# A graph kernel with two neural layers: message sums and gates in one rotation of five PSUM banks, one set of transposes issued a step later

## The chip, the cores and the metric

The kernel runs on one core of a Trainium2 chip. Times are microseconds on the device; the metric is the time of the core for one execution. One more execution was recorded by the hardware profiler, and all views below are of that one.

## What is computed

Sixteen graphs of 1024 nodes with 128 features each pass through two layers. Layer 0 is a gated recurrent network of four steps: messages are summed over the adjacency, and a GRU cell updates the node states. Layer 1 first thins the adjacency in a sequential rule (each row's removals change later rows), then runs three graph convolutions with batch norm. Both layers end with a residual and a layer norm. Cut to what matters here:

```python
h = x
for i in range(4):
    hw = einsum('bnc,cd->bnd', h, weight[i])
    m = einsum('bjn,bjd->bnd', adj, hw)
    h = gru_cell(m, h, w_ih[i], w_hh[i], b_ih[i], b_hh[i])   # gates r, z, n
# the thinning, for each row n in turn:
num = sum(row); rank = cumsum(row)
sf = where(num > 10, (num + 1) // 2, 1)
rm = row & (rank % sf == 0)            # removed in row n and in column n
```

## The kernel before, in words

The program has a first part, to about 1550 us, in which the gated network (class Gated) and the thinning (class FixPoint) run side by side, and a second part (class Sage) with the convolutions. The change touches the first part alone.

**Gated.** Two graphs are in flight as streams 0 and 1. run (L1083) loops over pairs of graphs, the four layers, and the two streams, and calls layer (L1033) each time: 64 calls. A layer holds nodes as columns, in two halves f=0 and f=1 of 512. For each half it sums messages into a PSUM bank (L1045): 8 matmuls with the high part of the state (hi) and 8 with the low part (lo), and ScalarE copies the sum to SBUF (h_ms, L1048). Then come the gates of each half (gate, L1054; matmuls L1057). Their order on TensorE: the reset gate r (weights on h, then on m), the hidden part ph (h), the input part px (m), the update gate z (h, then m). A float32 matmul of 128x512 is two instructions in the records, so a group of r or z has four. The readers: sigmoid of r on ScalarE (L1066), VectorE's product with ph (L1070) and sum with px (L1072), tanh on ScalarE (L1073), sigmoid of z on ScalarE (L1076), then z times h on GpSimd (L1078), VectorE (L1079) and GpSimd (L1080), which writes the new state. While one stream is in its layer, the other's new state is transposed (turn, L992, matmuls L997) and split into hi and lo (L985, L990).

**FixPoint.** It handles four graphs at a time (G = 4), in blocks of 128 rows: 32 blocks, k = 0 to 7 in each group of four graphs. It is a generator (steps, L735) with 20 yields to the block. For each graph g it needs the removals of earlier blocks, which are transposed on TensorE into the PSUM tile f_tr (turn, L716, matmuls L723; k of them, none where k = 0), multiplied into the rows on VectorE (L730), and counted by a scan of 1024 on VectorE (L732); L730 and L732 are in count (L725). There is one f_tr for all graphs, so the transposes of a graph wait for the multiply of the graph before, and a multiply waits for its transposes. After the four scans come the sum per row (L799), the parameters (L687 to L702), an Abs on ScalarE (diag_u, L870, L874), the removals x on VectorE (removed, L878, L881, tile f_x), and a triangular matmul on TensorE (less, L885, L889), whose result corrects the counts.

**The order.** [...] A layer calls aside(n) for n = 0 to 9, and each call takes one step of the generator, so a block of FixPoint lies on two calls of layer, stream 0 and then stream 1. In the second: aside 1 (between the hi and lo sums of f=0) issues the transposes and the count of graph 1; aside 2 (ahead of the hi sums of f=1) those transposes of graph 2; aside 3 (between hi and lo of f=1) the count of graph 2; aside 4 (after the sums) transposes and count of graph 3, L799, the parameters and diag_u. Then come r, ph and px of f=0, aside 5 (removed, and the other stream's turn), z of f=0, aside 6 (less), and the gates of f=1 with asides 7 to 9. Asides 2 and 3 are where the change moves a step. Graphs are counted from 0 here.

**PSUM.** Of the eight banks, FixPoint has two (f_tr and f_pd). Gated has three in the pool h_ps1 (the sums h_m0 and h_m1, and the transposes h_tr) and three in h_ps3, through which the eight gate groups of a layer rotate as h_g. A group may write a bank only after the reader of the group three before has ended: the z group of a half takes the bank of its own r group, and waits for that sigmoid.

Of the kernel before, what the change touches and what calls it, by code (L numbers as in the profile page):

```python
# [8 lines left out]
F32 = mybir.dt.float32  # L9
BF = mybir.dt.bfloat16  # L10
F16 = mybir.dt.float16
FR = mybir.dt.float32r
F8 = mybir.dt.float8e4
I32 = mybir.dt.int32
U8 = mybir.dt.uint8
AF = mybir.ActivationFunctionType
# [3 lines left out]
PSUM = bass.MemoryType.PSUM  # L20
# [5 lines left out]
C = 128  # L26
NB = N // P
HF = 512
# [24 lines left out]
class Dilate:  # L53
# [152 lines left out]
    def steps(self):  # L206

        for b in range(B):
            self.load(0, b)
            yield 3.0  # L210
        for k in range(NB):
            self.start_chain(k)
            for t in range(P):
                self.chain_step(k, t)
                yield 1.9
            self.end_chain(k)
            x = {}
            for i in range(B + 3):
                if i < B:
                    x[i] = self.rank(k, i)  # L220
                if 1 <= i <= B:
                    self.remove(k, i - 1, x.pop(i - 1))
                if i >= 3 and k + 1 < NB:
                    self.load(k + 1, i - 3)
                yield 5.0
# [402 lines left out]
class FixPoint:  # L628
# [106 lines left out]
    def steps(self):  # L735

        nc, G = self.nc, self.G
        for c in range(self.LOTS):
            self.load(c)
        old = None  # L740
        for i, (k, b0) in enumerate(self.todo):
            diag = slice(k * P, k * P + P)
            after = slice(k * P + 1, k * P + 1 + P)

            yield
            if old:
                old.settle()
                old.wide_u(0)
            yield
            if old:  # L750
                old.wide_u(1)
                old.rows(0)
            yield
            if old:
                old.wide_u(2)
                old.rows(1)
            yield
            if old:
                old.rows(2)
                old.wide_u(3)  # L760
            a = [self.loaded.pop((i, g)) for g in range(G)]
            pt = self.ps.tile([P, G, P], F32, name="f_pd")
            for g in range(G):
                nc.tensor.transpose(pt[:, g, :], a[g][:, diag], self.cst["ident"])
            yield
            yield
            if old:
                old.rows(3)
                old.last_u()
            yield  # L770

            self.turn(i, 0)
            yield

            both = self.small.tile([P, G, P], BF, name="f_both")
            for g in range(G):
                nc.vector.tensor_mul(both[:, g, :], a[g][:, diag], pt[:, g, :])
            nc.gpsimd.affine_select(both, both, pattern=[[0, G], [1, P]], compare_op=ALU.is_gt, fill=0.0,
                                    base=0, channel_multiplier=-1)
            rank = self.two.tile([P, G, N + 2], F16, name="f_rank")  # L780
            nc.vector.tensor_copy(rank[:, :, 0], self.first[:, k, b0:b0 + G])
            self.count(i, 0, a[0], rank, pt)
            yield
            yield
            yield
            self.turn(i, 1)
            self.count(i, 1, a[1], rank, pt)
            yield
            self.turn(i, 2)
            yield  # L790
            self.count(i, 2, a[2], rank, pt)
            for g in range(G):
                self.read_back(i + 1, g)
            yield
            self.turn(i, 3)
            self.count(i, 3, a[3], rank, pt)

            num = self.sm[:, 0, 0, :]
            nc.vector.tensor_scalar(num, rank[:, :, N], 1.0, None, op0=ALU.mult)  # L799
            q = self.params(num, 0)  # L800
            u = self.diag_u(rank[:, :, after], q)
            if old:
                old.check()
            yield
            x = self.removed(u, q, both)
            yield
            pd, num = self.less(x, rank, 1)
            rd = self.small.tile([P, G, P], F16, name="f_rd")
            q = self.params(num, 1, lambda: nc.vector.tensor_sub(rd, rank[:, :, after], pd))
            yield  # L810
            u = self.diag_u(rd, q)
            yield
            x = self.removed(u, q, both)
            yield
            old = self.Block(self, i, a, rank, both, x)
            yield
        for n in range(4):
            if n == 0:
                old.settle()
            old.wide_u(n)  # L820
            old.rows(n)
        old.last_u()
        old.check()
# [81 lines left out]
class Gated:  # L905
# [7 lines left out]
    def __init__(self, ctx, tc, cst, x, adj, weight, w_ih, w_hh, b_ih, b_hh, summed):  # L913
        self.tc, self.nc, self.cst = tc, tc.nc, cst
        self.x, self.adj, self.summed = x, adj, summed
        nc = self.nc
        pool = lambda name, **k: ctx.enter_context(tc.tile_pool(name=name, **k))
        self.one = pool("h_one", bufs=1)
        self.adjp = pool("h_adj", bufs=NB)
        self.wk = pool("h_wk", bufs=2)  # L920
        self.ps1 = pool("h_ps1", bufs=1, space=PSUM)
        self.ps3 = pool("h_ps3", bufs=3, space=PSUM)
        self.wi = self.one.tile([C, L0, 3, C], F32, name="h_wi")
        self.wh = self.one.tile([C, L0, 3, C], F32, name="h_wh")
        self.bi = self.one.tile([C, L0 * 3], F32, name="h_bi")
        self.bh = self.one.tile([C, L0 * 3], F32, name="h_bh")
        self.bs = self.one.tile([C, L0 * 3], F32, name="h_bs")
        with tc.tile_pool(name="h_in", bufs=2) as wk:
            self.prepare(wk, weight, w_ih, w_hh, b_ih, b_hh)
# [102 lines left out]

    def layer(self, st, l, aside):  # L1033

        nc, wk, ps1 = self.nc, self.wk, self.ps1
        half = [slice(f * HF, (f + 1) * HF) for f in range(2)]
        pm = [ps1.tile([C, HF], F32, name=f"h_m{f}") for f in range(2)]
        ms = []
        for f in range(2):
            for n, part in enumerate((st.hi, st.lo)):  # L1040
                aside(2 * f + n)
                if l == 0 and f == 1 and n == 0:
                    st.begin(1)
                for j in range(NB):
                    nc.tensor.matmul(pm[f], part[:, j, :], st.adj[j][:, half[f]],  # L1045
                                     start=(j == 0 and n == 0), stop=(j == NB - 1 and n == 1))
            m = wk.tile([C, HF], F32, name="h_ms")
            nc.scalar.copy(m, pm[f])  # L1048
            ms.append(m)
        aside(4)  # L1050
        bias = lambda t, g: t[:, 3 * l + g:3 * l + g + 1]
        w = lambda t, g: t[:, l, g, :]

        def gate(*mm):  # L1054
            pg = self.ps3.tile([C, HF], F32, name="h_g")
            for i, (lhs, rhs) in enumerate(mm):
                nc.tensor.matmul(pg, lhs, rhs, start=(i == 0), stop=(i == len(mm) - 1))  # L1057
            return pg

        for f in range(2):  # L1060
            h, m = st.ht[:, half[f]], ms[f]
            r = wk.tile([C, HF], F32, name="h_r")
            z = wk.tile([C, HF], F32, name="h_z")
            zh = wk.tile([C, HF], F32, name="h_zh")
            pr = gate((w(self.wh, 0), h), (w(self.wi, 0), m))
            nc.scalar.activation(r, pr, AF.Sigmoid, bias=bias(self.bs, 0))  # L1066
            if f == 1:
                aside(7)
            ph = gate((w(self.wh, 2), h))
            nc.vector.scalar_tensor_tensor(r, ph, bias(self.bh, 2), r, op0=ALU.add, op1=ALU.mult)  # L1070
            px = gate((w(self.wi, 2), m))
            nc.vector.tensor_add(r, px, r)  # L1072
            nc.scalar.activation(r, r, AF.Tanh, bias=bias(self.bi, 2))  # L1073
            aside(5 if f == 0 else 8)
            pz = gate((w(self.wh, 1), h), (w(self.wi, 1), m))
            nc.scalar.activation(z, pz, AF.Sigmoid, bias=bias(self.bs, 1))  # L1076

            nc.gpsimd.tensor_tensor(zh, z, h, ALU.mult)  # L1078
            nc.vector.scalar_tensor_tensor(r, z, 1.0, r, op0=ALU.subtract, op1=ALU.mult)  # L1079
            nc.gpsimd.tensor_tensor(h, zh, r, ALU.subtract)  # L1080
            aside(6 if f == 0 else 9)

    def run(self, steps):  # L1083
# [17 lines left out]
        for _ in steps:  # L1101
            pass

    def beside(self, st, ot, l, s, b0, steps):


# [815 lines left out]
```

## Time and profile before

| what | us |
|---|---|
| median of three runs | 2795.58 (2790.15 to 2797.11) |
| the profiled execution, its own time | 2790.13 |
| its span, first to last instruction | 2788.4 |
| TensorE matmul busy | 2420.7 (87%) |
| VectorE busy | 1972.3 (71%) |
| ScalarE busy | 1365.7 (49%) |
| GpSimd busy | 1007.0 (36%) |

The mean granted clock of TensorE is 0.951 of full speed. In a timeline line, the first number is the start in us from the first instruction, the second the length; then engine (PE is TensorE's matmul, PEld its weight load, DVE VectorE, ACT ScalarE, POOL GpSimd, SP the engine that only issues DMAs), line of the kernel, operation, tile written and tiles read, shapes, and how many were merged. Square brackets give the idle time of the engine just before and what ended it. In the windows view, PEclk is the granted clock of TensorE in that stretch.

### The profile page before, as it was taken

How to read it: one execution, taken by the hardware profiler on the slowest of the kernel's cores; microseconds unless marked ns; L12 is line 12 of the kernel's file. 1: busy time of each engine (PE TensorE's matmuls, PEld its weight loads, DVE VectorE, ACT ScalarE, POOL GpSimd, SP SyncE). 2: the span in 40 equal slices, each digit the busy share in tenths (PEclk: the TensorE clock that was granted, in tenths of full speed). 3: DMA queues.
4: the chain of work that ended last, by engine and by line, in shares of the span. 5: the costliest groups of instructions: out<-in, count | busy, mean ns of one | idle time of the engine just before them, and what ended most of it. 6: DMA issues, size and time to landing. Idle time of an engine off the chain costs nothing.

```text
span 2788.4 us, 35994 instructions
## 1 busy us (share of the span) xinstructions
PE 2420.7 (87%) x12167; PEld 1616.0 (58%) x12167; DVE 1972.3 (71%) x4184; ACT 1365.7 (49%) x3094; POOL 1007.0 (36%) x938
## 2 busy tenths in 40 slices
PE   5998989898989898989898599999999889988765
PEld 2555555555555555555554367767766677766544
DVE  1887887878878878788788656565566466656666
ACT  1455545454545454545554455555545344533335
POOL 2234334252352442533532454445445344430000
PEclk9999999999999999999999799999999999999986
DMA  6135344171342442623530757665666266643213
GB/s 223 48 129 175 106 149 146 50 251 59 132 166 94 152 149 69 218 71 128 176 103 27 295 201 253 247 229 214 250 242 225 96 225 225 232 164 107 92 38 100
DMA packets 214396, 436.19 MB, mean 156 GB/s; under 512 B 59573, under 2 KB 80730, under 8 KB 214202
## 3 DMA queue, kind: packets, MB, share of 16 engines
q1 hardware_dynamic: 191162, 349.91, 36.5%
q0 software_dynamic: 23040, 83.90, 9.0%
q8 instruction: 98, 1.61, 0.2%
q14 instruction: 96, 0.79, 0.1%
HBM read 324.49 MB, written 109.25 MB: 156 GB/s over the span
## 4 chain that ended last, share of the span: by engine, by line
DVE 37%; PE 29%; ACT 20%; DMA 6%; issue 5%; POOL 2%; SPq 0%; DVEq 0%; ACTq 0%; POOLq 0%
DVE f_rank L732 11%; PE h_g L1057 7%; PE p_ag L1477 6%; ACT s_junk L1317 3%; ACT f_pd L874 3%; DVE h_r L1079 3%; DVE f_a L730 2%; DVE s_r L1328 2%; PE p_dg L1461 2%; ACT f_u L897 2%; PE q_ag L1701 2%; ACT f_u L900 2%; DVE h_r L1070 2%; ACT h_r L1066 2%; DVE h_r L1072 2%
## 5 line engine op out<-in xcount | busy, mean ns | idle before, releaser
L1057 PE MATMUL h_g<-h_h,h_wh 128*128 128x512 f32 x768 | 429.0, 642 | 108.8 <-ACT h_r L1066 108.8
L1078 POOL TENSOR_TENSOR h_zh<-h_z,h_h 128x512 f32<-128x512 f32 x128 | 195.5, 1527 | 653.1 <-ACT h_z L1076 653.0
L1057 PE MATMUL h_g<-h_ms,h_wi 128*128 128x512 f32 x768 | 412.9, 621 | 0.0
L1409 POOL CAST p_b<-p_at 128x512 uint8<-128x512 f32 x256 | 213.0, 851 | 250.3 <-ACT p_at L1402 227.3
L732 DVE TENSOR_TENSOR_SCAN f_rank<-f_a,f_first,f_pd 128x1024 f16<-128x1024 f32 x128 | 299.8, 2347 | 4.0
L1045 PE MATMUL h_m<-h_a,h_hi 128*128 128x512 f32 x1024 | 281.7, 417 | 0.0
L1057 PEld LDWEIGHTS h_g<-h_ms,h_wi 128*128 128x128 f32 x768 | 154.3, 201 | 200.4 <-issue 194.6
L1045 PE MATMUL h_m<-h_a,h_lo 128*128 128x512 f32 x1024 | 260.4, 396 | 0.8 <-POOL h_lo L1017 0.7
L1402 ACT ACTIVATE p_at<-p_u,s_less 128x512 fp32r<-128x512 f32 x256 | 175.1, 685 | 157.0 <-PE p_u L1401 153.6
L1057 PEld LDWEIGHTS h_g<-h_h,h_wh 128*128 128x128 f32 x768 | 134.9, 201 | 198.1 <-ACT h_r L1066 126.8
L851 DVE SCALAR_TENSOR_TENSOR f_nr<-f_u,f_q,f_a 128x1024 bf16<-128x1024 f16 x128 | 195.3, 1528 | 56.7 <-ACT f_u L900 47.5
L1045 PEld LDWEIGHTS h_m<-h_a,h_hi 128*128 128x128 f32 x1024 | 189.4, 189 | 62.2 <-issue 27.4
L1080 POOL TENSOR_TENSOR h_h<-h_zh,h_r 128x512 f32<-128x512 f32 x128 | 190.2, 1486 | 73.8 <-DVE h_r L1079 51.0
L1317 ACT ACTIVATE s_junk<-s_o 128x128 bf16<-128x128 f32 x384 | 113.6, 298 | 204.5 <-DVE s_o L1310 204.5
L1045 PEld LDWEIGHTS h_m<-h_a,h_lo 128*128 128x128 f32 x1024 | 187.7, 188 | 39.1 <-POOL h_lo L1017 1.9
L1415 DVE SCALAR_TENSOR_TENSOR p_junk<-p_a 128x1024 bf16<-128x1024 f32 x128 | 183.9, 1437 | 2.3
L1070 DVE SCALAR_TENSOR_TENSOR h_r<-h_g,h_bh,h_r 128x512 f32<-128x512 f32 x128 | 95.7, 748 | 111.8 <-ACT h_r L1066 83.4
L1073 ACT ACTIVATE h_r<-h_r,h_bi 128x512 f32<-128x512 f32 x128 | 92.4, 722 | 163.4 <-DVE h_r L1072 163.4
L1048 ACT COPY h_ms<-h_m 128x512 f32<-128x512 f32 x128 | 73.7, 576 | 197.7 <-PE h_m L1045 156.8
L897 ACT ACTIVATE f_u<-f_rank,f_q 128x128 f16<-128x128 f16 (+7 forms) x128 | 110.6, 867 | 96.4 <-DVE f_rank L837 96.4
L1079 DVE SCALAR_TENSOR_TENSOR h_r<-h_z,h_r 128x512 f32<-128x512 f32 x128 | 118.2, 924 | 53.2 <-ACT h_z L1076 53.2
L1400 PE MATMUL p_u<-ident_b,p_a 128*128 128x128 bf16 x1024 | 146.8, 223 | 4.4 <-DMA p_a<-in_adj_dram 4.4
(227 smaller groups left out, 5072.6 us busy)
## 6 DMA issues: line engine op xcount, KB each, us to landing
h_a<-in_adj_dram POOLq DMA_DIRECT2D x128, 512.0 KB, 6.7
f_a<-in_adj_dram SPq DMA_DIRECT2D x128, 512.0 KB
p_a<-in_adj_dram SPq DMA_DIRECT2D x128, 512.0 KB
e_nr<-f_nr SPq DMA_DIRECT2D x128, 256.0 KB
p_nr<-e_nr SPq DMA_DIRECT2D x32, 1024.0 KB
s_at<-p_b SPq DMA_DIRECT2D x32, 512.0 KB
s_rt<-s_rt SPq DMA_DIRECT2D x64, 256.0 KB
s_ag<-s_ag SPq DMA_DIRECT2D x64, 256.0 KB
```

The source lines that it names most:

```text
L732: nc.vector.tensor_tensor_scan(out, a, other[:, 0, 0:1].to_broadcast([P, N]), start, op0=ALU.add, op1=ALU.bypass)
L851: nc.vector.scalar_tensor_tensor(nr, self.us[g], self.q[:, 2, g:g + 1], self.a[g], op0=ALU.not_equal, op1=ALU.is_ge)
L1045: nc.tensor.matmul(pm[f], part[:, j, :], st.adj[j][:, half[f]], start=(j == 0 and n == 0), stop=(j == NB - 1 and n == 1))
L1057: nc.tensor.matmul(pg, lhs, rhs, start=(i == 0), stop=(i == len(mm) - 1))
L1078: nc.gpsimd.tensor_tensor(zh, z, h, ALU.mult)
L1079: nc.vector.scalar_tensor_tensor(r, z, 1.0, r, op0=ALU.subtract, op1=ALU.mult)
L1080: nc.gpsimd.tensor_tensor(h, zh, r, ALU.subtract)
L1317: self.nc.scalar.activation(junk, o[:, i, :], AF.Square, accum_out=ss[:, i:i + 1])
L1402: nc.scalar.activation(g["at"][:, j, cols], pu, AF.Relu, bias=self.less2)
L1409: self.nc.gpsimd.tensor_copy(g["b", f][:, j, :], g["at"][:, j, f * HF:(f + 1) * HF].bitcast(F32))
L1415: self.nc.vector.scalar_tensor_tensor(junk, a, 0.0, a, op0=ALU.is_gt, op1=ALU.not_equal, accum_out=self.bad[:, c:c + 1])
L1477: self.nc.tensor.matmul(pa, hi[:, j, :], at[:, j, f * HF:(f + 1) * HF], start=(start and n == 0), stop=(stop and n == len(js) - 1))
```

## The change

The pools of the sums and of the gates become one: h_ps1 keeps only the bank of the transposes h_tr, and a pool h_ps5 of five banks serves both sums and all eight gate groups of a layer, ten allocations in the order m0, m1, r, ph, px, z (f=0), r, ph, px, z (f=1). Ten is twice five, so each use has the same bank in every layer: m0 and z of f=0 share one, m1 and r of f=1, r of f=0 and ph of f=1, ph of f=0 and px of f=1, px of f=0 and z of f=1. In FixPoint, the transposes of graph 2 move from aside 2 to aside 3, right ahead of the count that needs them. A constant that nothing uses goes too.

```diff
@@ FixPoint.steps
             self.turn(i, 1)
             self.count(i, 1, a[1], rank, pt)
             yield
+            yield
             self.turn(i, 2)
-            yield
             self.count(i, 2, a[2], rank, pt)
             for g in range(G):
                 self.read_back(i + 1, g)
@@ Gated.__init__
         self.ps1 = pool("h_ps1", bufs=1, space=PSUM)
-        self.ps3 = pool("h_ps3", bufs=3, space=PSUM)
+
+        self.ps5 = pool("h_ps5", bufs=5, space=PSUM)
@@ Gated.layer
-        nc, wk, ps1 = self.nc, self.wk, self.ps1
+        nc, wk = self.nc, self.wk
         half = [slice(f * HF, (f + 1) * HF) for f in range(2)]
-        pm = [ps1.tile([C, HF], F32, name=f"h_m{f}") for f in range(2)]
+        bank = lambda: self.ps5.tile([C, HF], F32, name="h_g")
+        pm = [bank() for f in range(2)]
         ms = []
@@
         def gate(*mm):
-            pg = self.ps3.tile([C, HF], F32, name="h_g")
+            pg = bank()
             for i, (lhs, rhs) in enumerate(mm):
```

More of the change, by code (lines that the diff above doesn't have):

```diff
@@ L12 @@
 FR = mybir.dt.float32r
-F8 = mybir.dt.float8e4
 I32 = mybir.dt.int32
```

## The prediction, made before the changed kernel was run

> **What bounds the kernel now.** The chain of the whole page came first: over the span it lies on several engines, none of which owns it.
>
> ```profile
> DVE 37%; PE 29%; ACT 20%; DMA 6%; issue 5%; POOL 2%; SPq 0%; DVEq 0%; ACTq 0%; POOLq 0%
> ```
>
> The change touches the first part alone (to about 1550 us), so next came the waits of TensorE between 50 and 1550 us. Columns: total us, times, longest.
>
> ```profile
> PE h_g L1057 <- ACT h_r L1066: 108.8, 41, 4.1
> PE f_tr L723 <- DVE f_a L730: 36.7, 33, 1.5
> ```
>
> These two are nearly all of TensorE's idle time there, 145.5 us, and the change aims at both. Whether removing them pays is read from one of the 32 fixed-point blocks. Its timeline:
>
> ```profile
> 635.52 1.95 ACT L874 ACTIVATE f_pd<-f_rank,f_q 128x128 f32<-128x128 f16 x4 [3.94 <-DVE f_q L698]
> 637.40 0.67 ACT L1066 ACTIVATE h_r<-h_g,h_bs 128x512 f32<-128x512 f32 x1
> 638.12 2.07 PE L1057 MATMUL h_g<-h_h,h_wh 128*128 128x512 f32 x2 [3.06 <-ACT h_r L1066]
> 639.57 1.12 DVE L881 SCALAR_TENSOR_TENSOR f_x<-f_pd,f_q,f_both 128x128 bf16<-128x128 f32 x4
> 641.70 0.63 PE L889 MATMUL f_pd<-f_tri,f_x 128*128 128x128 bf16 x4
> ```
>
> ScalarE stands 3.94 us before diag_u (L874), because VectorE's four scans are not done; the reset gate's sigmoid (L1066) is queued behind diag_u. TensorE's update-gate group wants that sigmoid's bank and waits 3.06 us. After this group comes less (L889), and it needs f_x, which VectorE ends at 639.57 + 1.12 = 640.69. That time hangs on the scans, diag_u, sigmoid, L1070, L1072 and L881, not on TensorE's update gate. The chain of waits runs through TensorE only from the restart on:
>
> ```profile
> 637.40 0.68 ACT h_r L1066
> ...
> 638.12 3.78 PE h_g L1057 x4
> 641.90 0.43 PE f_pd L889 x4
> 642.33 2.65 PE h_g L1057 x4
> ```
>
> The group took 3.78 us where the same four matmuls take 1.72 (0.43 each) elsewhere. In another block they ran at full speed, and less then waited for f_x:
>
> ```profile
> 314.82 1.13 PE L1057 MATMUL h_g<-h_h,h_wh 128*128 128x512 f32 x2 [3.59 <-ACT h_r L1066]
> 317.43 0.38 PE L889 MATMUL f_pd<-f_tri,f_x 128*128 128x128 bf16 x4 [0.63 <-DVE f_x L881]
> ```
>
> The windows view, cut at the edges where the granted clock can change (3.41 us apart, on one fixed grid), tells why. Columns: stretch, length, busy us of PE, PEld, DVE, ACT, POOL, then PEclk. First the block with the slow restart, then the other:
>
> ```profile
> 633.74:637.15 3.41, 1.33 (x7) 0.56 (x5) 3.24 (x13) 1.53 (x4) 0.00 (x0) 1.00 0.00 0
> 637.15:640.56 3.41, 2.44 (x3) 1.17 (x4) 2.73 (x8) 1.80 (x4) 0.00 (x0) 0.50 0.00 0
> 640.56:643.97 3.41, 3.41 (x9) 1.39 (x8) 2.05 (x9) 1.00 (x2) 1.26 (x1) 0.50 0.00 0
> ...
> 309.47:312.88 3.41, 1.75 (x8) 0.75 (x6) 3.27 (x10) 0.63 (x2) 0.00 (x0) 1.00 0.00 0
> 312.88:316.30 3.42, 1.48 (x4) 0.68 (x4) 2.71 (x8) 1.82 (x4) 0.00 (x0) 1.00 0.00 0
> ```
>
> A window with 2.08 us idle (3.41 - 1.33) was followed by half clock; one with 1.94 us idle was not. Over all windows of the first part the rule holds sharply: idle of 2.06 us or more halves the next window (25 windows), 1.98 or less never. A half window is followed by another if it had 0.59 us idle or more, and by full clock at 0.30 or less.
>
> [...]
>
> **What half clock costs now.** The start of the count's end (L799) marks each block. At the same place of the count, L799 to L799 is 43.70 us (from 451.38) and 43.70 (from 1198.22) with no half window, and 45.88 (from 825.69) with two. One place on: 44.16 with none (from 495.08), 45.06 with one (871.57), 46.41 with two (1241.92). So one window costs 0.9 us, two 2.2, and it comes through in full: from less to the next count TensorE is the path. Going through the 32 restarts: 8 at full clock, 15 with one half window, 9 with two. Taking 2.1 for two: 15 x 0.9 + 9 x 2.1 = 32.4 us lost of the profiled 2790.1.
>
> **The change, part by part.**
> 1. *Banks of the gates.* With ten allocations a layer over five banks, the update gate of f=0 takes the bank of the sum m0, whose copy (L1048) was done long before (654.22 against about 662). Every other group also finds its bank read: r0, ph, px of f=0 follow the other stream's last gates, r1 follows m1's copy, which it needs anyway. New bank waits: none, 0 us. The 108.8 us of waits go as waits. But the group merely runs at 635.1 to 636.8 instead of at 638.1, and then TensorE stands at less until f_x, about 640.74. Gain at less: its lateness behind f_x, 0 in a full-clock restart, about 1.0 in a two-window one (641.70 against 640.74). That is inside the 32.4 us. Bounds of other effects, such as the earlier sigmoid of z (ScalarE and VectorE each waited 1.06 us there at half clock): -0.3 to +0.3 us a block, since less and diag_u behind it hang on f_x and on the next reset gate; I take 0.
> 2. *Banks of the sums.* m0 now follows the update gate, m1 the reset gate of f=1 of the layer before, both read some 5 us earlier: 0.
> 3. *Third graph's transposes* (graph 2, counting from 0). Today they stand 1.28 us behind graph 1's multiply:
>
> ```profile
> 626.43 0.33 PE L723 MATMUL f_tr<-ident_b,f_rt 128*128 128x128 bf16 x3 [1.28 <-DVE f_a L730]
> 630.75 0.34 PE L723 MATMUL f_tr<-ident_b,f_rt 128*128 128x128 bf16 x3
> ```
>
> They move past eight sum matmuls (about 1.8 us); no DMA moves with them, and no queue of SP or POOL is passed. TensorE reaches them at about 627 and ends them by 627.5; the multiply that needs them starts at 628.7, when the scan ahead of it ends: cover 1.2 us, and VectorE would lose what exceeds it. Graph 3's transposes then come at 629.4 and meet a new wait, of 0 to 0.5 us, for graph 2's multiply (628.68 + 0.66); behind it stand only the gates of f=0, which have slack. VectorE's four scans, on the path, do not move: 0 us. But TensorE gets to its idle stretch some 1.0 us earlier.
>
> So TensorE's idle moves into one piece. From the end of the transposes (635.07) to f_x (640.74) is 5.67 us; less 1.72 of the update gate leaves 3.95; with 1.0 from edit 3, 4.9 (up to 5.7 late in the count, 4.1 in the blocks without transposes). Before it was 3.0 to 3.9, then 0.63.
>
> 4. *Half clock after the change.* With 4.9 us in one piece some window always has over 2 us idle, so no restart runs at full clock throughout. Let the restart fall p us after a grid edge, p anywhere in 3.41. p under 0.45 (13%): half to the next edge, 3.2 us on average. p from 0.45 to 3.0 (75%): half to the second edge, 6.83 - p, 5.1 on average. The rest (12%): one window, 3.41. Mean 0.42 + 3.83 + 0.41 = 4.65 us, in which 2.3 us of work is lost. All of it now falls on less and what follows; before, part fell on the update gate, while f_x was awaited anyway. For 31 blocks (the first has no long stall): 31 x 2.3 = 71.3 us.
>
> Sum: 71.3 - 32.4 = +38.9 us, 2829.0 on the profiled execution. That run lies 5.5 us under the median, and its 1.0 us lost a block is what the rule gives for its idle lengths, so it was not a lucky one in this. I add 38.9 to the mean of the profiled run and the three others, 2793.2: 2832.
>
> **Rivals.**
> - *Full clock at the restart (faster).* If TensorE's clock survived the idle stretch, less would start at f_x and all 32.4 us go: 2761. For: 8 of 32 restarts do it. Against: it needs under about 2.0 us idle in every window, and 4.1 to 5.7 us in one piece cannot give that. The plain reading, that all 145.5 us of waits go (2648), is part of this case and fails at less. Together 0.12.
> - *It cancels.* The restarts fall well on the grid, or ScalarE and VectorE hide part of the slow gates, and the lost time stays near 1.0 us a block: 2793. Against: the block lengths rise by the full lost work. 0.11.
> - *VectorE is held up too.* The moved transposes outlast their 1.2 us cover by 0.5 us in 28 blocks: 14 more, 2846. 0.05.
> - *Edit 1 does nothing*, the waits staying where they are; edit 3 alone then lengthens the idle by 1.0 us, from some 3.3 to 4.3. By the same rule 1.4 us a block: 31 x 0.4 = 12 more than now, 2805. 0.04.
>
> **Numbers.** The likeliest case has 0.68; alone it runs from 2813 (1.7 us a block) to 2850. About 0.3% (8 us) is what a measurement of this kernel tells from no change. Faster 0.12, within 0.11, slower 0.68 + 0.05 + 0.04 = 0.77. The range reaches into the cancelling case, 2796, and to 2851 for the held-up VectorE; about 0.2 is left out, mostly the faster case.
>
> **What would show it.** Right: the wait on L1066 gone from TensorE; in its place less (L889) waiting for f_x (L881), 4 to 5.7 us a time, some 150 us in all; waits of L723 down from 36.7 to about 10; L799 to L799 longer by about 1.3 us; mean granted clock some 0.93 to 0.94 instead of 0.951. Wrong: restarts at full clock, less starting earlier than f_x allows now, or scans that begin earlier within a block.

## The result, and the profile after

The changed kernel takes 2813.71 us (median of four runs, 2810.86 to 2814.44) against 2796.35 us before (four runs, 2790.15 to 2802.3): a ratio of 1.006, 95% interval 1.0037 to 1.0084. It is slower, by 17.4 us. The forecast was slower by 39, from 2793 to 2832: the direction came, the size was more than twice too large. The profiled execution took 2813.35 us, with a span of 2811.6. Lines of Gated lie one further down in the changed file, those of FixPoint one further up.

TensorE's waits between 50 and 1560 us (total us, times, longest):

```profile
PE f_pd L888 <- DVE f_x L880: 162.5, 32, 5.6
PE f_tr L722 <- DVE f_a L729: 8.4, 16, 0.7
```

Both old waits went as planned: the 108.8 us on the sigmoid are gone, the 36.7 us before the transposes are down to 8.4. They came back at less, 162.5 us, 5.1 on average. The block whose restart the prediction took apart (the 13th), in the timeline of the changed kernel:

```profile
644.69 1.02 PE L1058 MATMUL h_g<-h_ms,h_wi 128*128 128x512 f32 x2
650.98 0.59 PE L888 MATMUL f_pd<-f_tri,f_x 128*128 128x128 bf16 x4 [5.26 <-DVE f_x L880]
651.36 2.02 PE L1058 MATMUL h_g<-h_h,h_wh 128*128 128x512 f32 x2
...
645.76 1.95 ACT L873 ACTIVATE f_pd<-f_rank,f_q 128x128 f32<-128x128 f16 x4 [5.25 <-DVE f_q L697]
647.64 0.67 ACT L1067 ACTIVATE h_r<-h_g,h_bs 128x512 f32<-128x512 f32 x1
```

The update gate ends by 645.7, ahead of the sigmoid that it used to wait for. Then TensorE stands still for 5.26 us, and the next gate runs at half speed: two instructions in 2.02 us where a pair takes 1.02. The windows view in steps of 3.41 us, of which the trace has 443 between 40 and 1560 us, every one at a granted clock of 1.00 or 0.50 and none between (columns as in the prediction; the last two, of DMA, play no part here):

```profile
642.21:645.63 3.42, 3.42 (x12) 1.43 (x10) 3.28 (x7) 0.00 (x0) 0.00 (x0) 1.00 0.00 0
645.63:649.04 3.41, 0.08 (x1) 0.00 (x0) 2.77 (x10) 2.45 (x5) 0.00 (x0) 1.00 0.00 0
649.04:652.45 3.41, 1.47 (x6) 1.06 (x7) 3.08 (x9) 1.78 (x3) 0.66 (x1) 0.50 0.00 0
652.45:655.87 3.42, 3.42 (x9) 1.76 (x8) 1.43 (x8) 0.69 (x2) 2.38 (x2) 0.50 0.00 0
655.87:659.28 3.41, 3.41 (x10) 1.50 (x9) 2.23 (x5) 2.98 (x6) 0.00 (x0) 1.00 0.00 0
```

The window with 0.08 us of work was followed by two at half clock. All 31 restarts after the first block meet half clock, where 7 of these came through before (8 of 32 with the first block); the mean granted clock fell from 0.951 to 0.936. And the chain of waits of the whole page leans on TensorE more than before (29%):

```profile
PE 40%; DVE 35%; ACT 14%; DMA 5%; issue 4%; POOL 1%; SPq 0%; DVEq 0%; ACTq 0%; POOLq 0%
```

### The profile page after: what moved, and what is told of

Same layout as the page of the kernel before. It is cut to its first block, busy times and chain, and to the rows that moved or that the text cites. A ratio compares the mean times of both kernels' runs of the same rounds, so it can differ in the third digit from the quotient of the medians.

```text
span 2811.6 us, 35977 instructions
## 1 busy us (share of the span) xinstructions
PE 2426.0 (86%) x12150; PEld 1630.7 (58%) x12167; DVE 1958.7 (70%) x4184; ACT 1367.9 (49%) x3094; POOL 1018.2 (36%) x938
## 4 chain that ended last, share of the span: by engine, by line
PE 40%; DVE 35%; ACT 14%; DMA 5%; issue 4%; POOL 1%; SPq 0%; DVEq 0%; ACTq 0%; POOLq 0%
PE h_g L1058 11%; DVE f_rank L731 11%; PE h_g L1046 6%; PE p_ag L1478 6%; ACT s_junk L1318 3%; DVE f_a L729 2%; DVE s_r L1329 2%; PE p_dg L1462 2%; PE q_ag L1702 2%; DVE f_nr L850 2%; DVE h_r L1073 2%; DVE h_r L1071 2%; ACT f_pd L873 2%; DMA p_a<-in_adj_dram 2%; DVE h_r L1080 2%
## 5 line engine op out<-in xcount | busy, mean ns | idle before, releaser
L1079 POOL TENSOR_TENSOR h_zh<-h_z,h_h 128x512 f32<-128x512 f32 x128 | 205.2, 1603 | 678.4 <-ACT h_z L1077 678.3
L1058 PE MATMUL h_g<-h_h,h_wh 128*128 128x512 f32 x768 | 426.8, 639 | 0.0
L1058 PE MATMUL h_g<-h_ms,h_wi 128*128 128x512 f32 x768 | 415.6, 624 | 0.0
L1046 PE MATMUL h_g<-h_a,h_hi 128*128 128x512 f32 x1024 | 278.5, 414 | 0.0
L1058 PEld LDWEIGHTS h_g<-h_ms,h_wi 128*128 128x128 f32 x768 | 155.0, 202 | 201.4 <-issue 200.4
L1046 PE MATMUL h_g<-h_a,h_lo 128*128 128x512 f32 x1024 | 263.5, 399 | 1.5 <-POOL h_lo L1017 1.5
L1046 PEld LDWEIGHTS h_g<-h_a,h_hi 128*128 128x128 f32 x1024 | 190.8, 189 | 59.4 <-issue 21.5
L1046 PEld LDWEIGHTS h_g<-h_a,h_lo 128*128 128x128 f32 x1024 | 185.7, 188 | 37.9 <-POOL h_lo L1017 2.4
L1058 PEld LDWEIGHTS h_g<-h_h,h_wh 128*128 128x128 f32 x768 | 139.0, 206 | 77.8 <-issue 75.8
L888 PE MATMUL f_pd<-f_tri,f_x 128*128 128x128 bf16 x256 | 31.4, 261 | 162.5 <-DVE f_x L880 162.5
L1049 ACT COPY h_ms<-h_g 128x512 f32<-128x512 f32 x128 | 73.9, 577 | 174.8 <-PE h_g L1046 162.0
```

## The experiments

The theory under test: what the change costs is half clock after one long idle piece; the two edits are otherwise free. The rivals: the moved transposes hold VectorE up, or the clock is not what the path feels. Every median below is set against runs of the kernel before on the same chip; these were 2795.91 (22 runs, 2786.38 to 2805.07) for the first four, 2797.01 (11) for the next four and 2798.26 (19) for the last two. The changed kernel's own 2813.71 stands beside a median of 2796.35, so a difference between a run here and the changed kernel is good to some 2 us.

**The banks alone.** The transposes go back to their place:

```diff
             yield
-            yield
             self.turn(i, 2)
+            yield
             self.count(i, 2, a[2], rank, pt)
```

> The five-bank rotation alone; the third graph's transposes stay where they were. Half-clock theory: TensorE's idle before less is one piece of about 4.0 us (5.06 in the changed kernel, less the 1.0 that the transposes' wait takes back), every restart still meets a half window, and the time is near the changed kernel's: 2803 to 2815. Rival, the moved transposes are what costs (they hold up VectorE): no slower than before, 2796 or less.

Measured: 2808.91, ratio 1.0055 (1.0036 to 1.0074). As the theory had it. TensorE's waits:

```profile
PE f_pd L888 <- DVE f_x L880: 135.5, 32, 5.0
PE f_tr L722 <- DVE f_a L729: 34.9, 32, 1.5
```

With 4.2 us idle at less on average (135.5 / 32), 30 of the 31 restarts met half clock. The banks alone do most of the harm, 13 us.

**The transposes alone.** The same edit made in the kernel before.

> The moved transposes alone, with the old banks. Half-clock theory: the wait of the update gate for the reset gate's sigmoid grows from some 3.3 to some 4.3 us, fewer restarts come through at full clock, 0.4 us a block: about 2806. Rival, VectorE held up by the transposes: the multiply of graph 2 starts late behind its scan, and the time is that of the changed kernel, 2814, with the scans further apart. Rival, the move is free: 2796.

Measured: 2801.88, ratio 1.0025 (1.0013 to 1.0037), 6 us over before. TensorE's waits:

```profile
PE h_g L1057 <- ACT h_r L1066: 137.5, 41, 4.7
PE f_tr L723 <- DVE f_a L730: 8.1, 17, 0.8
```

28.6 us left the second wait and 28.7 came to the first: time that TensorE saves there turns into a longer stand at the sigmoid. The distance from the first scan of a block to L799 is the same to 0.1 us with and without the move (12.67 us at k = 6 in all three kernels), so VectorE is not held up, and that rival falls. The forecast of 2806 was high by 4 us: the profiled execution of this run, 2802.33, lies 12.2 us over that of the kernel before, just as forecast, but that one was a quick execution of its kernel, as is found below.

**Spare matmuls.** To keep the clock up without touching anything else, TensorE is given matmuls whose result is overwritten, ahead of the update gate where it would stand idle:

```diff
-        def gate(*mm):
+        def gate(*mm, spare=0):
             pg = bank()
+            for _ in range(spare):
+                nc.tensor.matmul(pg, *mm[0], start=True, stop=True)
...
-            pz = gate((w(self.wh, 1), h), (w(self.wi, 1), m))
+            spare = 4 if f == 0 and ot == 1 else 0
+            pz = gate((w(self.wh, 1), h), (w(self.wi, 1), m), spare=spare)
```

(ot is the number of the stream, handed to layer.) Nothing of the computation is left out. In the runs with spares the lines of Gated lie a little further down: the gate matmuls of L1058 are L1060 here and L1061 in the last run, the reset gate's sigmoid, L1067, is L1069 and L1070. With four:

> The changed kernel with four spare matmuls of 0.86 us (their result is overwritten) ahead of the update gate of f=0 of the second stream: TensorE's idle before less falls from 5.06 to about 1.6 us, under the 2.0 us that halve a window. Half-clock theory: all restarts at full clock, the changed kernel's 63 us of lost work go in full (2750) or, if part of that loss was hidden by other engines, in the greater part (2760). Rival, the clock is not what the path feels (VectorE and ScalarE set the block): the time stays near 2814, or grows with the added work.

Measured: 2774.42, ratio 0.9927 (0.9908 to 0.9945). More work on TensorE, and 39 us less than the changed kernel: the clock is what the path feels. It fell short of 2750 to 2760, and the profile shows where. Two restarts, one with 1.83 us idle before less, one with 1.96, with the clock's windows at each:

```profile
638.39 0.38 PE L888 MATMUL f_pd<-f_tri,f_x 128*128 128x128 bf16 x4 [1.83 <-DVE f_x L880]
638.62 1.08 PE L1060 MATMUL h_g<-h_h,h_wh 128*128 128x512 f32 x2
...
684.32 0.38 PE L888 MATMUL f_pd<-f_tri,f_x 128*128 128x128 bf16 x4 [1.96 <-DVE f_x L880]
684.54 1.57 PE L1060 MATMUL h_g<-h_h,h_wh 128*128 128x512 f32 x2
```

```profile
633.79:637.20 3.41, 2.78 (x7) 0.95 (x5) 2.70 (x7) 1.87 (x4) 0.00 (x0) 1.00 0.00 0
637.20:640.62 3.42, 2.23 (x11) 1.31 (x12) 3.12 (x13) 1.78 (x3) 1.42 (x1) 1.00 0.00 0
...
681.58:684.99 3.41, 1.45 (x7) 0.56 (x6) 2.97 (x7) 1.79 (x4) 0.00 (x0) 1.00 0.00 0
684.99:688.40 3.41, 3.41 (x8) 1.68 (x7) 2.23 (x10) 0.55 (x2) 3.04 (x2) 0.50 0.00 0
```

The first idle piece lies across an edge, 0.63 us idle in one window and 1.19 in the next, and both windows and the gates behind it are at full clock (two instructions in 1.08 us); the second falls into one window whole, 3.41 - 1.45 = 1.96 us, and the next is at 0.50. Eight restarts late in the count were hit so, for some 9 us in all, and the four spares delayed the first block's less by 1.5 us, since it has no long stand. The rest of the shortfall is the hidden part explained below.

With two instead of four:

> The same with two spare matmuls: idle of about 3.3 us in one piece, so that some restarts have a half window and some none. Half-clock theory: between the two, about 1.6 us lost a block instead of 2.05, near 2800. Rival, the spare matmuls help or hurt in proportion to their number: half of what four do.

Measured: 2803.1, ratio 1.003 (1.0013 to 1.0047). Two spares save 10.6 us, four save 39.3: not in proportion to their number. With two, 3.4 us are left on average and 26 of the 31 restarts still meet a half window; with four, 1.8 us and 8. With five spares, none in the first block:

> The changed kernel with five spare matmuls instead of four, none in the first block (where they delayed less by 1.5 us). TensorE's idle before less: 0.7 to 1.3 us. Half-clock theory: no half window at any restart, the 11 us that eight half windows still cost with four go, and the first block's 1.5: 2762. Rival, the remaining difference had other causes, or the fifth begins to delay less: 2774 or more.

Measured: 2765.22, ratio 0.9885 (0.987 to 0.99). No restart meets a half window now, with 1.0 us idle at less on average (31.2 us in 32 waits, the longest 1.8); 48.5 us less than the changed kernel. And five spares with the transposes in their old place:

> Five banks and five spare matmuls, the third graph's transposes back in their old place: the idle left before less is under 0.7 us. Half-clock theory, with the transposes off the path at full clock: the same time as with the moved transposes, 2762 (within 4). Rival, the moved transposes save something of their own: slower by up to the 1.0 us a block in which they advance TensorE, 2790.

Measured: 2764.93, ratio 0.9886 (0.987 to 0.9901), the same time. At full clock the moved transposes are worth nothing that these runs can tell.

**The next graph's x, earlier.** The load goes out up to a layer before:

```diff
             if old:
                 jobs[5].append(lambda: ot.finish(0))
                 jobs[7].append(lambda: ot.finish(1))
-                jobs[0] = [lambda: ot.load_x(nxt)]
...
         if l == L0 - 1:
             for j in range(4):
                 jobs.setdefault(4, []).append(lambda j=j: st.load_adj(st.b + 2, j))
+            jobs.setdefault(8 if s else 4, []).append(lambda: st.load_x(st.b + 2))
```

> The changed kernel with the load of the next graph's x issued up to a layer earlier, in the same three buffers. Theory of where lost time was hidden: in the seven blocks that open a new pair of graphs ScalarE's split waits for that load, about 3.9 us a time, and half clock costs little there (0.2 to 1.1 us instead of about 2). With the load early these blocks get 2 to 3.5 us shorter and now pay the half clock in full: 2813 less 14 to 25, near 2795. Rival, the load is not what bounds them: no change, 2813.

Measured: 2810.96, ratio 1.0051 (1.0037 to 1.0064). And with five spares:

> Early load and five spare matmuls. Theory: the gains add, and the blocks that open a pair gain more than in the run without spares, by the half clock that was hidden there, about 1 us each: 2762 less 20 to 32, near 2737. Rival, the two overlap: 2750 or more.

Measured: 2764.35, ratio 0.9882 (0.9867 to 0.9897). Both theories failed, and the times are those of their rivals; the seven blocks that open a pair got at most 0.4 us shorter at full clock (four of them 48.6 to 48.9 us instead of 48.8 to 49.0, three 45.7 to 46.0 instead of 46.0 to 46.4). The chain of waits of the second run says why:

```profile
958.76 1.30 POOL h_x L1029
960.05 0.29 issue
960.34 2.97 DMA e_sum<-h_x
...
963.87 4.49 DMA h_x<-in_x_dram
```

With three buffers, one load still waits until the finished graph's sum has been stored from its buffer: it starts 18.1 us after that block's L798 with and without the edit. The other stream's load does go out earlier, by some 17 us, and that brings little. A fourth buffer was not tried. Whether the load is what bounds those blocks stays open.

**The reset gate's sigmoid ahead of diag_u.** In the second stream's layer, the step of aside 4 is issued after the reset gate and its sigmoid. ScalarE then does the sigmoid in the time it would wait for diag_u's parameters.

```diff
-        aside(4)
+        if ot == 0:
+            aside(4)
...
             nc.scalar.activation(r, pr, AF.Sigmoid, bias=bias(self.bs, 0))
             if f == 1:
                 aside(7)
+            elif ot == 1:
+                aside(4)
```

Alone, in the changed kernel:

> The changed kernel with that order alone, no spare matmuls: TensorE's idle before less falls from 5.06 to about 4.4 us, which still halves the clock at every restart. Half-clock theory: only the 20 us of the earlier f_x, 2794. Rival, the order itself cures the idling: 2770 or less.

Measured: 2798.84, ratio 1.0003 (0.9994 to 1.0013), 15 us less than the changed kernel, where 20 were expected. In its trace the half clock after less lasts 4.6 us on average, in that of the changed kernel 4.2, which may have taken the rest. With four spare matmuls:

> Five banks, moved transposes, four spare matmuls (none in the first block), and in the second stream's layer the step of aside 4 (the last count, the parameters, diag_u) issued after the reset gate of f=0 and its sigmoid instead of ahead of them. ScalarE then does the sigmoid while it would wait for diag_u's parameters, so f_x is ready about 0.65 us earlier. Theory, that less hangs on f_x and the path on less: 0.65 us x 31 = 20 us off the run with five spares, 2745. Rival, another chain takes over: 2760 to 2765.

Measured: 2747.97, ratio 0.982 (0.9805 to 0.9835): 17 us less than the run with five spares, and 50 us less than the runs of the kernel before beside it. One block of it, ScalarE first, then VectorE:

```profile
661.79 0.69 ACT L1070 ACTIVATE h_r<-h_g,h_bs 128x512 f32<-128x512 f32 x1 [1.14 <-PE h_g L1061]
666.67 1.95 ACT L873 ACTIVATE f_pd<-f_rank,f_q 128x128 f32<-128x128 f16 x4 [4.20 <-DVE f_q L697]
...
665.87 0.17 DVE L798 TENSOR_SCALAR f_tr<-f_rank 128x4 f32<-128x4 f16 x1
670.06 1.12 DVE L880 SCALAR_TENSOR_TENSOR f_x<-f_pd,f_q,f_both 128x128 bf16<-128x128 f32 x4
```

f_x starts 4.19 us after L798, where it started 4.85 after L799 before (639.57 against 634.72). At full clock all of these 0.66 us reach the end: from L798 to L798 the first three places of the count take 43.05, 43.49 and 43.92 us (from 441.92, 484.97 and 528.45), with five spares alone 43.71, 44.14 and 44.57. So f_x is on the path, as the prediction's steps 1 and 4 took it. That only 17 us came of the expected 20 has a cause in the clock: with four spares six restarts late in the count met a half window again, and two of these blocks are 1.6 us longer for it. Five spares with this order were not run. It is the fastest version here.

## Why the prediction was right or wrong

*Steps 1 and 2, the banks: right.* No group waits for a bank any more, and less starts 0.05 us after f_x in every block. The stand that was forecast as 4.9 us, up to 5.7 late in the count, measures 5.1 on average and 5.6 at most. The rival that edit 1 does nothing, and the one that all waits go, fall.

*Step 3, the transposes: right.* No hold on VectorE; the new wait for graph 2's multiply is within the 8.4 us that is left of all waits of L722.

*Step 4, half clock: right in mechanism, wrong in size.* This is the step that failed. Its sum was 71.3 - 32.4 = +38.9; measured, it is 48.8 - 23.5 = +25.3. Most of the error lies in "it comes through in full": the prediction let all lost work reach the end, and 14.7 us of it do not. Each term can be set against the run with five spares, where no window is halved and L798 to L798 repeats to 0.1 us at nearly every place of the count: 43.71, 44.14, 44.56, 45.58, 46.10 and 46.64 us, and about 49.0 and 46.1 where a new pair of graphs is opened. (Of the eight blocks of the kernel before that met no half window, seven have the same lengths, 43.7, 44.15, 45.57 and 46.11, and one is 0.2 us longer: the spares do nothing to such a block but keep its clock.)

- *Length of the half clock after less.* Taken as 4.65 us on average, with restarts anywhere on the grid. Measured 4.23 over the 30 restarts up to the last count, so 63.5 us of work lost, not 71.3 (which had counted the last restart too, for 2.3). Short and long cases came as forecast (8 of 30 with 3.41 us or less), but the long ones average 4.7, not 5.1. The restarts do not fall anywhere on the grid: the block lengths repeat, and with them the phases.
- *How much of it reaches the end.* Taken as all. Measured: the 31 distances from L798 to L798 add up to 1466.3 us, at full clock to 1417.5, so 48.8 us reach the end and 14.7 are hidden. The rival "It cancels" had named this, that other engines hide part of the slow gates; it was turned down because block lengths rise by the full lost work, which had been read at two places of the count, neither of them in a block that opens a pair. Half of the hidden time, 7.7 us, is in the seven blocks that do. So TensorE has about 1 us to spare there, and at full clock (five spares) the chain of waits of such a block runs through GpSimd, the load of x and ScalarE:

```profile
963.49 1.00 POOL h_h L1084
964.48 0.52 issue
965.00 4.83 DMA h_x<-in_x_dram
969.86 0.99 ACT h_hi L1016 x2
```

  The other half, 0.3 us a block, is everywhere else. Take the 22nd block, in the changed kernel and then with five spares:

```profile
1071.48 0.17 DVE L798 TENSOR_SCALAR f_tr<-f_rank 128x4 f32<-128x4 f16 x1
1119.79 0.17 DVE L798 TENSOR_SCALAR f_tr<-f_rank 128x4 f32<-128x4 f16 x1
...
1041.43 0.17 DVE L798 TENSOR_SCALAR f_tr<-f_rank 128x4 f32<-128x4 f16 x1
1087.53 0.17 DVE L798 TENSOR_SCALAR f_tr<-f_rank 128x4 f32<-128x4 f16 x1
```

  In the gates of the next layer TensorE is 2.47 us later than with five spares, which is what its half clock of 5.03 us predicts; but L798 to L798 is 48.31 against 46.10, 2.21 longer. The chain of waits of both kernels in that stretch, the changed one first:

```profile
1094.06 3.44 PE h_g L1058 x8
1097.50 0.44 PE h_tr L997 x4
1097.93 1.73 PE h_g L1058 x4
1099.67 0.02 issue
1099.69 0.70 ACT h_z L1077
```

```profile
1062.72 0.59 ACT f_u L896
1063.31 0.24 issue
1063.55 0.59 ACT f_u L899
1064.14 0.58 ACT h_r L1069
1064.72 0.03 issue
1064.75 0.76 DVE h_r L1073
```

At half clock TensorE's gates are the chain; at full clock it is ScalarE's queue of f_u and the sigmoid. The prediction said that from less to the next count TensorE is the path. In this block it is so only once TensorE is late by 0.3 us.

- *What the kernel before lost already.* Taken as 32.4 us, 2.1 of it for the last restart, after which there is no count. Up to the last count it is 23.5 (1441.0 against 1417.5). The blocks that open a pair make nearly all of the difference: they were taken at 8.7 us and lost 2.3.

So the first part grew by 25.3 us up to its last count, where 38.9 was forecast: 14.7 too much for what is hidden and 5.5 for the length of the half clock, less 6.8 by which the old loss was overstated; the last restarts make up 0.2. From there to the end the changed kernel takes 2.1 us less (1264.3 against 1266.3), which makes the 23.2 us between the two profiled executions. Only about 0.4 us of these 2.1 come in the first part; the others arise in the second, which the change leaves alone, and say nothing of it.

*The step from the profiled execution to the median: wrong.* "It was not a lucky one in this" failed. Over 22 runs the kernel before spreads from 2786 to 2805, and its profiled run, at 2790.1, lies about 6 us under their middle, while the changed kernel's lies at its own. That takes 23.2 to 17.4: the profiled execution of before was a lucky one. The granted clock of those 22 runs goes with their time, 0.950 to 0.953 in the four quickest, 0.942 in the three slowest. So it is likely, though only one execution of each kernel was traced, that the restarts of the kernel before meet the grid differently from run to run. In the changed one every restart is hit, and its four runs lie within 4 us.

*Why the old profile looked like a gain.* 145 us of TensorE's waits stood in the way of nothing: VectorE's scans, diag_u and the sigmoid decide when f_x is ready, and less waits for it (162.5 us in the changed kernel). Removing the wait ahead of that point joined the idle into one piece: 3.06 us at the sigmoid in the 13th block before, 5.26 at less after.

## What to carry to other kernels

A wait of TensorE that was taken away here, ahead of another that ends later, saved no time; it made the later idle piece longer, 5.1 us on average, and the longer piece cost again, in half clock after it: at 31 restarts of 32 instead of 24, and the first part took 25.3 us more. So ask what TensorE does between the freed wait and the next one, how long it will then stand in one piece, and who has slack when it comes back slow. Where the stand had to stay, spare matmuls that filled it were worth 39 us (four, which left 1.8 us idle on average) and 48 (five, 1.0 us) here; two, which left 3.4 us, only 11; and the move of one sigmoid ahead of a blocked instruction 15 to 17.

## What the runs showed of the hardware

Idle is counted here as the prediction counts it, from the busy time of PE in the windows view. In windows of 3.41 us, cut in steps of 3.4133 us from 640.56 in the kernel before and from 649.04 in the changed one, the granted clock is 1.00 or 0.50 in all 444 and 443 windows between 40 and 1560 us. In the kernel before, all 25 full-clock windows with 2.06 us idle or more were followed by one at 0.50, and none of those with 1.98 or less; in the changed one all 31 with 2.04 or more, and none of those with 1.47 or less. With four spares one with 1.96 us idle was followed by one at 0.50 (681.58, above), and with two spares one with 2.01 us by full clock:

```profile
743.52:746.93 3.41, 1.40 (x7) 0.94 (x8) 3.08 (x9) 1.78 (x3) 0.59 (x1) 1.00 0.01 2
746.93:750.35 3.42, 3.42 (x12) 1.72 (x11) 2.64 (x11) 2.46 (x6) 2.46 (x2) 1.00 0.00 0
```

So between 1.96 and 2.01 us these records have both cases, and they tell no more. Of the windows at 0.50, one with 0.68 us idle was followed by full clock in the changed kernel, one with 0.59 us by another at 0.50 in the kernel before:

```profile
222.37:225.78 3.41, 2.73 (x7) 1.49 (x7) 2.01 (x6) 1.96 (x6) 1.95 (x2) 0.50 0.97 351
225.78:229.19 3.41, 3.41 (x12) 1.72 (x11) 2.46 (x9) 2.45 (x6) 2.26 (x2) 1.00 0.01 2
...
1244.73:1248.14 3.41, 2.82 (x4) 1.27 (x5) 2.51 (x7) 1.73 (x3) 0.00 (x0) 0.50 0.00 0
1248.14:1251.55 3.41, 3.41 (x9) 1.60 (x8) 2.28 (x8) 0.69 (x1) 1.65 (x1) 0.50 0.02 5
```

In the kernel before alone, full clock had followed only half windows with 0.30 us idle or less.
